# Two graph-attention layers and a binarized layer on one core: new places for three vector and scalar operations within a step, and a third buffer for the 8-bit adjacency blocks

## The chip, the cores and the metric

The kernel runs on one core of a Trainium2 chip. The metric is device time in microseconds (us) of one execution, taken as the median of several runs. A profiled execution of the same program gives the trace that the prediction is read from. Engines are named as the profile names them: PE (TensorE; PEld is its weight load), DVE (VectorE), ACT (ScalarE), POOL (GpSimd), SP (the queue that issues most DMAs).

## The reference

`x` has 3327 rows of 512 numbers, `adj` is a 3327 by 3327 matrix of zeros and ones. Two graph-attention layers run one after the other, then layer norm, then a layer on signs, then layer norm again.

```python
def _gat_layer(x, W, adj):
    proj = x @ W
    Wh, Ws = jnp.split(proj, 2, axis=-1)
    scores = Wh @ Ws.T
    a = jax.nn.softmax(scores, axis=-1) * adj
    out = a @ Wh
    out = out + x
    return jax.nn.leaky_relu(out, NEG_SLOPE)
...
# layer 0: x = layernorm(x + gat(gat(x)));  layer 1:
bw = sign(weight); ba = maximum(sign(x), 0)
out = relu(adj @ (ba @ bw.T))
x = layernorm(x + out)
```

## The kernel before

**Tiling.** The 3327 rows make 26 tiles of 128, taken in pairs: 13 pairs. An attention layer is a walk over 169 steps `(g, q)`: `g` is the pair of query rows, `q` the pair of key rows. Scores are computed transposed, keys on the 128 partitions, so that a step's block of scores is one tile `s` of 128 x 512 (two halves of 128 x 256). The function `attention` (L707) is called once for each of the two layers (`l` 0 and 1).

**What a step does.** The loop over `v` (L1348) writes the instructions of one step into all queues. A step works on several blocks at once, since the work on a block is a pipeline: scores are computed 31 steps ahead, and in step `v`

- `shift` (L1041, DVE L1044) subtracts the query rows' maximum from the block of step `v+3`. The maximum lies in a PSUM tile, `beside`, which `spread` (L1038, an ACT copy) fills once a group `g`;
- `exponential` (L1046, ACT L1050; for a group's first block also L1049 into `total`) follows on the same block;
- `running` (L1052, DVE L1055) adds the block of step `v+2` to the group's running total; a group's first block needs no addition;
- `masked` (L1057, DVE L1060) multiplies the block of step `v+2` by its adjacency block and calls `sums` (L1088), four subtractions and additions on POOL (L1093 to L1096) that prepare the Strassen-like product;
- `values` (L1104) multiplies the block of step `v` by the values on PE (L1120, 14 matmul instructions);
- `scores` (L881) or `quad_scores` (L786) compute a part of the scores of later blocks on PE;
- each layer also makes an 8-bit copy of half of the adjacency blocks (`narrow` L1063, ACT L1068, into a tile of tag `adj_b` with 2 buffers), counts degrees (`degrees`, POOL L1073), checks that the entries are zeros and ones (`exact`, DVE L1083) and, in the next step, stores the copy (`keep_blocks`, a DMA issued by POOL, L1076). In most of a layer this is every other step; a few places in between take a further block (`room`, L1341), so that there three steps in a row have one.

**The order by hand.** Every piece of a step is put on a list `work` with a place in the step, a number between 0 and 1 (L1370 to L1399), the list is sorted by it (L1400) and written out. The sort sets the order of the instructions on each engine's queue; each engine then works through its queue in order and waits where something is not ready. So a place is no time: it says only what stands ahead of what on the same engine. Places over 1 go to later steps through the table `early`.

**The scores by blocks of 26 products.** For most key rows the scores come from `quad_scores`: one block of 26 products of 128 x 128 by 128 x 256 (L820, two matmul instructions each) for four steps, interleaved with the matmuls of `values`. The products are numbered in `ORDER` and have the places `(n + 0.5) / 6.5` for n = 0 to 25. They accumulate in PSUM banks `P`, `Q`, `R`, later `S`, `T`, `V`; `ps_ch` has three of them. A bank is read out between two products on it, by ACT (`keep_as`, L826, and `seed`, L829, which writes one back) or by DVE (`out`, L832), and the next product on the bank waits for that reading. DVE's readings have the place of their product plus 0.082, ACT's plus 0.03. There are five such blocks in a pass of 26 steps (two groups), five passes of that kind and 25 blocks in each layer. The steps of a block have different readings: in its first step DVE has product 16 (place 0.774), in the second 12 and 9 (0.082 and 0.236), in the third 21, 7, 24, 6 (0.31, 0.467, 0.62, 0.774), in the fourth 15, 18, 5, 10, 17, 2 (0.082, 0.236, 0.39, 0.544, 0.70, 0.852). ACT's readings fall in the first two steps and early in the third. `maximum` (L868, DVE L879) keeps the running maximum over keys, with places such as 0.49 and 0.79. For the first and last key rows of a pass the scores come from `scores` instead, with products on banks `Z`, `Y`, `X` (L781), ACT copies (L897, L902, L926, L930) and DVE additions (L916, L922).

**The maximum over partitions.** `column_max` (L951) folds a group's maximum in five pieces (`fold`, `turn`, `across`, `along`, `back`) that a table of places, `plans` (L937), spreads over steps.

Of the kernel before, what the change touches and what calls it, by code (L numbers as in the profile page):

```python
# [11 lines left out]
F8 = mybir.dt.float8e4  # L12
# [7 lines left out]
P = 128  # L20
# [3 lines left out]
HW = CW // 2  # L24
# [21 lines left out]
def kernel(  # L46
# [24 lines left out]
    def halves_of(c):  # L71
        return [g for g in (2 * c, 2 * c + 1) if g < NQ]

    def dense(c):
        return 0 < c and len(halves_of(c)) == 2 and c < NC
# [20 lines left out]
    def slot(shape, dtype, name):  # L96
        return ring.tile(shape, dtype, tag="s", bufs=SBUFS, name=name)
# [609 lines left out]
    def attention(l, att):  # L707
# [67 lines left out]
        def product(c, q, bank, a, b, start):  # L775

            if start:
                w = len(halves_of(c)) * P
                ch[bank] = ps_ch.tile([P, w], F32, tag="ch", name=f"p{bank}_{l}_{c}_{q}")
            for k in range(2):  # L780
                nc.tensor.matmul(  # L781
                    ch[bank], xs[c, q, a][:, k], query(c, b)[:, k],
                    start=(start and k == 0), stop=(k == 1), skip_group_check=True,
                )
# [96 lines left out]
        def scores(c, q, s):  # L881

            if dense(c) and q // 2 in quads:
                if (q % 2, s) == (0, 0):
                    quad_scores(c, q // 2)
                return []
            mine = halves_of(c)
            if s == 0:
                for i in mine:
                    sc[i, q] = slot([P, 2, HW], F32, f"s_{l}_{i}_{q}")  # L890
            w = len(mine) * P
            lo, hi = sc[mine[0], q][:, :, :w], sc[mine[-1], q][:, :, HW - w :]
            c11, c21, c12, c22 = lo[:, 0], lo[:, 1], hi[:, 0], hi[:, 1]

            def copied(name, bank):
                ch[name] = att.tile([P, w], F32, tag=name, bufs=1, name=f"{name}_{l}_{c}_{q}")
                nc.scalar.copy(ch[name], ch[bank])  # L897

            def z1():
                product(c, q, "Z", A11, B11, True)  # L900
                ch["X"] = ps_ch.tile([P, w], F32, tag="ch", name=f"pX_{l}_{c}_{q}")
                nc.scalar.copy(ch["X"], ch["Z"])  # L902

            def y5():
                product(c, q, "Y", S1, T1, True)
                copied("p5", "Y")

            def z6():
                product(c, q, "Z", S2, T2, False)
                copied("u2", "Z")  # L910

            def y3():
                product(c, q, "Y", S4, B22, False)

            def add12():
                nc.vector.tensor_tensor(c12, ch["Y"], ch["u2"], ALU.add)  # L916

            def z7():
                product(c, q, "Z", S3, T3, False)

            def add22():
                nc.vector.tensor_tensor(c22, ch["Z"], ch["p5"], ALU.add)  # L922

            def x2():
                product(c, q, "X", A12, B21, False)
                nc.scalar.copy(c11, ch["X"])  # L926

            def z4():
                product(c, q, "Z", A22, T4, False)
                nc.scalar.copy(c21, ch["Z"])  # L930

            if s == 1:

                after.append((-0.05, lambda: maximum(mine[0], q)))
                if q == NQ - 1:

                    plans = [  # L937
                        ((1, -0.04), (1, 0.2), (1, 0.6), (2, 0.16), (2, 0.17)) if mine[0] == 0
                        else ((1, -0.04), (1, 0.2), (1, 0.7), (2, 0.02), (2, 0.3)),
                        ((2, 0.68), (5, 0.83), (6, 0.83), (7, 0.83), (8, 0.83)),  # L940
                    ]
                    for i, plan in zip(mine, plans):
                        for (n, at), do in zip(plan, column_max(i)):
                            early.setdefault(v + n, []).append((at, do))
            if s == 0:
                return [(0.06, z1), (0.31, y5), (0.56, z6), (0.81, y3), (0.94, add12)]
            return [
                (0.02, z7), (0.15, add22), (0.35, x2), (0.68, z4),
            ] + [(0.62, lambda i=i: maximum(i, q)) for i in mine[1:]]
# [91 lines left out]
        def shift(g, q):  # L1041
            s = sc[g, q]
            at = beside[l][:, 0:1]
            nc.vector.tensor_tensor(s, s, at.to_broadcast([P, 2, HW]), ALU.subtract)  # L1044

        def exponential(g, q):  # L1046
            if q == 0:
                total[g] = att.tile([P, 2, HW], F32, tag="total", name=f"total_{l}_{g}")
                nc.scalar.activation(total[g], sc[g, q], AF.Exp)  # L1049
            nc.scalar.activation(sc[g, q], sc[g, q], AF.Exp)  # L1050

        def running(g, q):  # L1052

            if q > 0:
                nc.vector.tensor_tensor(total[g], total[g], sc[g, q], ALU.add)  # L1055

        def masked(g, q):  # L1057

            s = sc[g, q]
            nc.vector.tensor_tensor(s, s, adj[g, q], ALU.mult)  # L1060
            sums(g, q, s)

        def narrow(g, q):  # L1063

            t = adj[g, q, "b"] = att.tile(
                [P, 2, HW], F8, tag="adj_b", bufs=2, name=f"ab_{l}_{g}_{q}"
            )
            nc.scalar.copy(t, adj[g, q], saturate=False)  # L1068

# [192 lines left out]
        if last:  # L1262
# [14 lines left out]
            for n, e in enumerate(some):  # L1277
                at = n * (n1 - n0) / len(some)
# [59 lines left out]
        mine = [i for i, e in enumerate(steps) if e[1] % L == l]  # L1338
# [9 lines left out]
        for v in range(-LOOK - 4, len(steps)):  # L1348
            u = v + LOOK

            if 0 <= v + WS - 1 < len(steps):
                load_ws(*steps[v + WS - 1])
            if 0 <= v + 4 < len(steps):
                load_adj(*steps[v + 4])
            if v + 4 in blocks and (v + 4 < 0 or blocks[v + 4] != steps[v + 4]):
                load_adj(*blocks[v + 4])
            if 0 <= u + 2 < len(ahead):
                c, q, h = ahead[u + 2]
                if h == 0:
                    load_xs(c, q)  # L1360
            if u == -4:
                load_gs(0, 0, 7)

            c, i = divmod(u, 2 * NQ)
            if 0 <= c < NC - 1 and 22 <= i < 25:
                load_gs(c + 1, 2 * i - 44, 1 if i == 24 else 2)
            if dense(c) and i == 0 and quads:
                for n, at, do in query_sums(c):
                    early.setdefault(v + n, []).append((at, do))
            work, after = after, []  # L1370
            if 0 <= c < NC - 1 and i == 2 * NQ - 1:
                work += [
                    (at, lambda c=c, n=n: load_gs(c + 1, n)) for n, at in ((5, 0.43), (6, 0.8))
                ]
            if 0 <= v + 3 < len(steps):
                s3 = steps[v + 3]
                if not any(s3):
                    work.append((-0.02, lambda: spread(0)))
                at = 0.12 if v >= 0 else 0.33 if v < -2 else 0.45
                work += [(0.0, lambda: shift(*s3)), (at, lambda: exponential(*s3))]  # L1380
                if s3[1] == NQ - 1 and s3[0] + 1 < NQ:
                    work.append((0.9, lambda: spread(s3[0] + 1)))
            if 0 <= v + 2 < len(steps):
                s2 = steps[v + 2]
                work += [(0.2, lambda: running(*s2)), (0.48, lambda: masked(*s2))]
            if v + 2 in blocks:
                of = blocks[v + 2]
                work += [
                    (0.6, lambda: narrow(*of)), (0.61, lambda: degrees(*of)),
                    (0.66, lambda: exact(*of)),  # L1390
                ]
                after.append((0.5, lambda of=of: keep_blocks(*of)))
            if later and (last or v + 2 not in blocks or len(later) > 5 - v % NQ // 2):
                work += [(0.8, later.pop(0))]
            if 0 <= u < len(ahead):
                work += scores(*ahead[u])
            if v >= 0:
                work += values(*steps[v])
            work += early.get(v, [])  # L1399
            for _, do in sorted(work, key=lambda e: e[0]):  # L1400
                do()
            if v >= 0 and steps[v][1] == NQ - 1:
                later += finish(steps[v][0])
            if last:
                load_products(v)
# [337 lines left out]
```

## Time and profile before

| | us |
|---|---|
| median of 3 runs | 2499.78 (2499.44 to 2500.13) |
| the profiled execution, its own time | 2498.87 |
| span of that execution, first to last instruction | 2497.1 |
| PE busy in the span | 2471.4 |
| DVE busy | 2031.8 |
| POOL busy | 1505.6 |
| ACT busy | 852.9 |

| group | times | mean ns | busy us |
|---|---|---|---|
| L1044 shift, DVE | 338 | 674 | 227.7 |
| L1050 exponential, ACT | 338 | 631 | 213.2 |
| L1055 running total, DVE | 312 | 844 | 263.4 |
| L1060 masking, DVE | 338 | 717 | 242.5 |
| L879 maximum, DVE | 286 | 786 | 224.0 |
| L1068 8-bit copy, ACT | 169 | 617 | 104.3 |
| L1076 its store, issued by POOL | 169 | 556 | 94.0 |

The first table has whole times; the busy time of an engine is the union of its instructions' records. The second has instructions by line; "mean ns" is the mean length of one record. The granted TensorE clock is 0.999 of full speed over the whole execution.

### The profile page before, as it was taken

How to read it: one execution, taken by the hardware profiler on the slowest of the kernel's cores; microseconds unless marked ns; L12 is line 12 of the kernel's file. 1: busy time of each engine (PE TensorE's matmuls, PEld its weight loads, DVE VectorE, ACT ScalarE, POOL GpSimd, SP SyncE). 2: the span in 40 equal slices, each digit the busy share in tenths (PEclk: the TensorE clock that was granted, in tenths of full speed). 3: DMA queues.
4: the chain of work that ended last, by engine and by line, in shares of the span. 5: the costliest groups of instructions: out<-in, count | busy, mean ns of one | idle time of the engine just before them, and what ended most of it. 6: DMA issues, size and time to landing. Idle time of an engine off the chain costs nothing.

```text
span 2497.1 us, 39159 instructions
## 1 busy us (share of the span) xinstructions
PE 2471.4 (99%) x12052; PEld 2140.4 (86%) x12052; DVE 2031.8 (81%) x4005; ACT 852.9 (34%) x2127; POOL 1505.6 (60%) x2487
## 2 busy tenths in 40 slices
PE   9999999999999999999999999999999999999998
PEld 7888888888888888998888888888888888899886
DVE  6864788888988988768886588988889898888876
ACT  3333433333333333322233333333333333332234
POOL 3772566767677676545677256666666666655631
PEclk9999999999999999999999999999999999999999
DMA  6976767676677766897797676767767677688985
GB/s 209 322 267 222 249 236 253 233 262 236 239 253 236 266 230 231 294 317 258 244 334 270 225 260 220 269 223 265 241 232 270 227 268 240 230 283 301 317 279 174
DMA packets 318149, 635.89 MB, mean 255 GB/s; under 512 B 34317, under 2 KB 182405, under 8 KB 317934
## 3 DMA queue, kind: packets, MB, share of 16 engines
q1 hardware_dynamic: 289454, 540.93, 64.9%
q0 software_dynamic: 28480, 92.40, 9.6%
q8 instruction: 98, 1.61, 0.3%
q14 instruction: 117, 0.96, 0.1%
HBM read 521.98 MB, written 111.21 MB: 254 GB/s over the span
## 4 chain that ended last, share of the span: by engine, by line
PE 93%; DVE 4%; DMA 1%; issue 1%; ACT 1%; POOL 0%; SPq 0%; ACTq 0%; DVEq 0%; POOLq 0%
PE acc L1120 38%; PE pZ L781 9%; PE pP L820 6%; PE pQ L820 6%; PE pY L781 5%; PE pR L820 4%; PE pZ_wh L547 4%; PE pZ_g L612 3%; PE agg L1471 3%; PE pX L781 2%; PE pY_wh L547 2%; PE pY_g L612 2%; PE pT L820 2%; PE pS L820 1%; PE pm L439 1%; PE pV L820 1%
## 5 line engine op out<-in xcount | busy, mean ns | idle before, releaser
L1093 POOL TENSOR_TENSOR as<-s 128x128 f32<-128x128 f32 x338 | 210.9, 624 | 563.3 <-DVE s L1060 424.6
L1120 PE MATMUL acc<-ws,s 128*128 128x256 f32 x1352 | 402.3, 379 | 0.0
L1120 PE MATMUL acc<-ws,as 128*128 128x256 f32 x1352 | 380.5, 379 | 0.0
L1120 PE MATMUL acc<-wh,s 128*128 128x256 f32 x1352 | 380.0, 379 | 0.0
L1050 ACT ACTIVATE s<-s 128x512 f32<-128x512 f32 x338 | 213.2, 631 | 399.5 <-DVE s L1044 397.6
L1073 POOL TENSOR_TENSOR deg<-deg,adj 128x256 fp8e4<-128x256 fp8e4 x338 | 263.6, 780 | 44.5 <-DMA adj<-in_adjT_dram 29.7
L1120 PEld LDWEIGHTS acc<-ws,as 128*128 128x128 f32 x1352 | 251.4, 190 | 37.0 <-issue 3.1
L1120 PEld LDWEIGHTS acc<-wh,s 128*128 128x128 f32 x1352 | 252.5, 190 | 32.5
L1120 PEld LDWEIGHTS acc<-ws,s 128*128 128x128 f32 x1352 | 251.4, 190 | 33.1
L1055 DVE TENSOR_TENSOR total<-total,s 128x512 f32<-128x512 f32 x312 | 263.4, 844 | 0.0
L1060 DVE TENSOR_TENSOR s<-s,adj 128x512 f32<-128x512 f32 x338 | 242.5, 717 | 2.6 <-DMA adj<-in_adjT_dram 0.3
L879 DVE TENSOR_TENSOR top<-top,s 128x512 f32<-128x512 f32 x286 | 224.0, 786 | 23.4 <-ACT s L930 21.3
L781 PE MATMUL pZ<-ga,xs 128*128 128x256 f32 (+1 forms) x1096 | 234.3, 340 | 2.1 <-DVE s L922 1.7
L1044 DVE TENSOR_TENSOR s<-s,beside 128x512 f32<-128x512 f32 x338 | 227.7, 674 | 2.5 <-ACT beside L1039 2.5
L1094 POOL TENSOR_TENSOR s<-s 128x128 f32<-128x128 f32 x338 | 207.4, 614 | 26.7
L781 PEld LDWEIGHTS pZ<-ga,xs 128*128 128x128 f32 x1096 | 191.4, 190 | 26.4 <-DVE s L922 2.5
L1095 POOL TENSOR_TENSOR as<-s 128x128 f32<-128x128 f32 x338 | 191.3, 566 | 26.5
L1096 POOL TENSOR_TENSOR as<-s,as 128x128 f32<-128x128 f32 x338 | 185.3, 548 | 26.5
L1120 PE MATMUL acc<-wh,as 128*128 128x256 f32 x676 | 201.2, 379 | 0.0
L826 ACT COPY s<-pP 128x256 f32<-128x256 f32 x200 | 74.3, 372 | 249.6 <-PE pP L820 217.3
L1120 PEld LDWEIGHTS acc<-wh,as 128*128 128x128 f32 x676 | 125.7, 190 | 20.2 <-issue 3.6
L1076 POOL DMA_DIRECT2D adj_d<-ab x169 | 94.0, 556 | 78.5 <-ACT ab L1068 58.0
(274 smaller groups left out, 4969.6 us busy)
## 6 DMA issues: line engine op xcount, KB each, us to landing
ws<-ws_d SPq DMA_DIRECT2D x338, 512.0 KB
adj<-in_adjT_dram SPq DMA_DIRECT2D x351, 256.0 KB
xs<-xq_d SPq DMA_DIRECT2D x100, 832.0 KB
xs<-xs_d SPq DMA_DIRECT2D x82, 512.0 KB
xs<-xs_d SPq DMA_DIRECT2D x82, 384.0 KB
gs_d<-gsp POOLq DMA_DIRECT2D x84, 256.0 KB, 3.8
xq_d<-xq POOLq DMA_DIRECT2D x20, 832.0 KB, 4.7
ga<-gs_d SPq DMA_DIRECT2D x54, 256.0 KB
```

The lines of the kernel that those rows point to most:

```text
L781: nc.tensor.matmul(ch[bank], xs[c, q, a][:, k], query(c, b)[:, k], start=(start and k == 0), stop=(k == 1), skip_group_check=True,)
L820: nc.tensor.matmul(bank[b], xs[c, i, f"x{r}"], right, start=r in begins, stop=True, skip_group_check=True,)
L879: nc.vector.tensor_tensor(top[i], top[i], t, ALU.max)
L1044: nc.vector.tensor_tensor(s, s, at.to_broadcast([P, 2, HW]), ALU.subtract)
L1050: nc.scalar.activation(sc[g, q], sc[g, q], AF.Exp)
L1055: nc.vector.tensor_tensor(total[g], total[g], sc[g, q], ALU.add)
L1060: nc.vector.tensor_tensor(s, s, adj[g, q], ALU.mult)
L1073: nc.gpsimd.tensor_tensor(deg[:, g], deg[:, g], adj[g, q][:, a], ALU.add, saturate=False)
L1093: nc.gpsimd.tensor_tensor(s3, a11, a21, ALU.subtract)
L1094: nc.gpsimd.tensor_tensor(a21, a21, a22, ALU.add)
L1095: nc.gpsimd.tensor_tensor(s2, a21, a11, ALU.subtract)
L1120: nc.tensor.matmul(acc[g][i // 2][:, i % 2], a[i], b[i], start=(q == 0 and i % 2 == 0), stop=(q == NQ - 1), skip_group_check=True,)
```

## The change

Four edits. In `attention`'s step loop `shift` goes from place 0.0 to 0.25, `exponential` from 0.12 (0.33 and 0.45 in the three steps ahead of the first) to 0.75 in all steps, `running` from 0.2 to 0.475, directly ahead of `masked` at 0.48. The tile of the 8-bit copies gets a third buffer. In `plans`, the third piece (`across`) of a layer's first group goes from 0.6 to 0.97 of its step. What is computed is the same.

```diff
-                        ((1, -0.04), (1, 0.2), (1, 0.6), (2, 0.16), (2, 0.17)) if mine[0] == 0
+                        ((1, -0.04), (1, 0.2), (1, 0.97), (2, 0.16), (2, 0.17)) if mine[0] == 0
...
             t = adj[g, q, "b"] = att.tile(
-                [P, 2, HW], F8, tag="adj_b", bufs=2, name=f"ab_{l}_{g}_{q}"
+                [P, 2, HW], F8, tag="adj_b", bufs=3, name=f"ab_{l}_{g}_{q}"
             )
...
-                at = 0.12 if v >= 0 else 0.33 if v < -2 else 0.45
-                work += [(0.0, lambda: shift(*s3)), (at, lambda: exponential(*s3))]
+                work += [(0.25, lambda: shift(*s3)), (0.75, lambda: exponential(*s3))]
                 if s3[1] == NQ - 1 and s3[0] + 1 < NQ:
                     work.append((0.9, lambda: spread(s3[0] + 1)))
             if 0 <= v + 2 < len(steps):
                 s2 = steps[v + 2]
-                work += [(0.2, lambda: running(*s2)), (0.48, lambda: masked(*s2))]
+                work += [(0.475, lambda: running(*s2)), (0.48, lambda: masked(*s2))]
```

## The prediction

> **What bounds the kernel.** I read the page first: span, busy shares, the chain that ended last.
>
> ```profile
> span 2497.1 us, 39159 instructions
> PE 2471.4 (99%) x12052; PEld 2140.4 (86%) x12052; DVE 2031.8 (81%) x4005; ACT 852.9 (34%) x2127; POOL 1505.6 (60%) x2487
> PE 93%; DVE 4%; DMA 1%; issue 1%; ACT 1%; POOL 0%; SPq 0%; ACTq 0%; DVEq 0%; POOLq 0%
> ```
>
> PE sets the end; the three operations that move run on DVE and ACT and count only where PE waits for what stands behind them. So the question is how much PE waits, and the busy share hides that: the record of a matmul lasts longer (379 ns for 128x256) than the distance to the next one. The busy time by window tells it by counts, in the middle of layer 0 and of layer 1.
>
> ```profile
> 312.00:1000.00 688.00, 687.66 (x3193) 603.70 (x3192) 598.51 (x1179) 244.07 (x590) 467.23 (x741) 1.00 0.72 243
> 1500.00:2187.00 687.00, 681.23 (x3129) 588.48 (x3128) 606.68 (x1213) 233.01 (x567) 441.59 (x709) 1.00 0.71 245
> ```
>
> The first window has 3193 matmuls in 688 us, 0.2155 us each. At that rate 687 us hold 3188; layer 1 has 3129. The 59 that are missing are 12.7 us of waits, though PE looks busy for 681.23. That is the sum to be won in layer 1; layer 0's steady part has next to none. The first steps of each layer lose more (the slices 250:312.5 and 1437.5:1500 have 272 and 271 matmuls where 291 fit, some 4.2 us each).
>
> Then the tables of waits, PE's and all engines':
>
> ```profile
> PE pP L820 <- DVE s L832: 2.3, 6, 0.4
> PE pQ L820 <- ACT s L826: 2.2, 2, 1.5
> PE pP L820 <- ACT s L826: 2.0, 2, 1.3
> ...
> ACT s L1050 <- DVE s L1044: 397.6, 197, 6.5
> ACT ab L1068 <- DMA adj_d<-ab: 40.0, 17, 4.4
> ```
>
> PE waits where a score bank has not been read out, by DVE or ACT. ACT stands idle 397.6 us in the exponential until DVE has shifted, and 40.0 us in the 8-bit copy until an earlier store has landed; readings queued behind are late. The timeline shows both ways to PE. First the buffer:
>
> ```profile
> 1667.26 0.59 PE L1120 MATMUL acc<-wh,s 128*128 128x256 f32 x2
> ...
> 1668.43 0.62 ACT L1068 CAST ab<-adj 128x512 fp8e4<-128x512 f32 x1 [4.00 <-DMA adj_d<-ab]
> 1668.96 0.36 ACT L826 COPY s<-pQ 128x256 f32<-128x256 f32 x1
> 1669.38 0.70 PE L820 MATMUL pQ<-gb,xs 128*128 128x256 f32 x2 [1.52 <-ACT s L826]
> ```
>
> ACT sat 4.00 us in the copy for a buffer, then read bank Q at 1668.96, and PE's next product on Q, due 0.43 after 1667.26 (two matmuls), came at 1669.38: 1.69 lost. Then the order on DVE, at the start of the third step of a pass's fourth block, layer 1:
>
> ```profile
> 1541.47 0.67 DVE L1044 TENSOR_TENSOR s<-s,beside 128x512 f32<-128x512 f32 x1
> 1541.50 0.59 PE L820 MATMUL pP<-ga,xs 128*128 128x256 f32 x2
> ...
> 1542.06 1.02 DVE L1055 TENSOR_TENSOR total<-total,s 128x512 f32<-128x512 f32 x1
> ...
> 1543.35 0.41 DVE L832 TENSOR_TENSOR s<-pP,s 128x256 f32<-128x256 f32 x1
> ...
> 1543.81 0.70 PE L820 MATMUL pP<-gb,xs 128*128 128x256 f32 x2 [0.42 <-DVE s L832]
> ```
>
> Product 7 on bank P starts at 1541.50; its sum can be read 0.70 later (1542.20) but DVE first shifts and adds to the running total and reads P at 1543.35. The next product on P is only two pitches of 0.86 behind, due at 1543.22: 0.59 lost.
>
> **The parts.** (a) Third buffer. A copy then waits for the store of three copies ago; with one copy a step that is a step, some 5.8 us, more than the longest wait (4.4). Two waits of PE come of it: 1.69 and, at 2114.00, 0.85 (idle 0.68 and 0.17 of hidden pitch). **-2.5**. The ACT and DVE time freed beside it (DVE idles 21.6 us behind these copies) has no other wait of PE.
>
> (b) Shift to 0.25, exponential to 0.75. On ACT the exponential no longer stands ahead of a step's first readings while DVE is late. Worth: one wait of bank Y (1593.31, 0.67 idle + 0.16) and two of bank Z at the layers' starts (0.35 each): **-1.5**. The two waits of bank P for ACT (2.0 us) get no credit: the product after them waits for DVE's reading of product 16 anyway, whose place stays behind shift, total and masking. Costs: the exponential now stands behind the 8-bit copy (0.6) and ahead of ACT's readings at 0.876 and, a step later, 0.80 and 0.95. Copy and exponential are 1.25 us together; in the first step they run between the results of products 23 and 14, in the second a reading comes 0.2 late of the 1.4 that a bank allows (three pitches 2.58, less 0.70 to the result, 0.37 for the copy, 0.1). A group's first block has 0.63 more: still inside. The exponential ends by the end of its step at worst, the total reads it at 0.475 of the next, 2.7 us later. Nothing: 0; without that slack each exponential that is late would cost its lateness once, on DVE.
>
> (c) Total behind the readings below 0.475. Before masking DVE does the same work as before, so no reading is put later while DVE has a backlog; those below 0.25 gain shift and total (0.60 + 0.60 to 1.0), those from 0.25 to 0.475 the total. At 1541 the change gives: shift to 1542.06, reading of Q to 1542.40, of P to 1542.82, in time. Then total (0.60 to 1.02), masking 0.60, maximum 0.60, so the reading of S starts 1544.54 to 1544.96 and ends 0.42 later, against 1544.94, when S is wanted: 0.1 to 0.5 lost instead, I take 0.3. From a block's first product row to its last takes 22.02 us undisturbed; these fourth blocks take 22.92 in all five passes: 5 x (0.90 - 0.30) = -3.0. First blocks of passes two to five take 22.83 to 23.01, because the readings of 12 and 9 stand behind shift and total and the copies-out of a finished group: both now go ahead, -0.83 x 4 = -3.3. The second and third blocks lose some 3 more in readings 15 and 18, which gain, but reading 10 behind them gets no earlier: 0, bounds 0 and -3. **-6.3**.
>
> (d) Where DVE has no backlog the same order costs. Layer 0, third step of a second block:
>
> ```profile
> 617.57 0.68 DVE L1044 TENSOR_TENSOR s<-s,beside 128x512 f32<-128x512 f32 x1
> 618.16 0.87 DVE L1055 TENSOR_TENSOR total<-total,s 128x512 f32<-128x512 f32 x1
> 619.61 0.42 DVE L832 TENSOR_TENSOR s<-pQ,s 128x256 f32<-128x256 f32 x1 [0.58 <-PE pQ L820]
> 620.54 0.42 DVE L832 TENSOR_TENSOR s<-pP,s 128x256 f32<-128x256 f32 x1 [0.51 <-ACT pQ L829]
> 622.09 0.42 DVE L832 TENSOR_TENSOR qu<-pS,qu 128x256 f32<-128x256 f32 x1
> ```
>
> DVE had shifted and added before the results came and then idled 0.58 and 0.51. Now the total waits behind the reading at 620.54, and total, masking and maximum run as one before that of 622.09. This starts at 622.69 with the total at 0.60, ends 623.11, and PE wants S at 623.29: 0.13 to spare after 0.05 for the signal. The reading after it (622.42) has 0.7 to spare, 0.06 where the check of the entries stands between. With the total at its 1.02 of 1542.06 the first is 0.3 late. 35 blocks have this form (the second to fifth of each five, 40 of 50, less the five above): 0 to 10.5. Nearest row: masking, whose place it joins, has a mean of 717 against the total's 844; so mostly 0.60, and I take **+2**.
>
> A rule of the Trainium skill bears on this: "SBUF — State Buffer", section "SBUF: two separate sides", has DVE operations with two SBUF inputs and GpSimd operations that read SBUF shut each other out for a whole instruction. The trace agrees: the total (both inputs in SBUF) has 664/701/1658 ns as minimum, median and maximum, the shift (one in PSUM) 636/675/690. By it the total runs free where POOL waits for the masking, and (d) would be 0; if POOL's degree count still ran there, (d) would go to its upper end.
>
> (e) `across` moves behind the addition L916 but stays ahead of L922, for which PE waits at 268.18; the work ahead of that is the same: 0. If L922 gained, it would be 0.9 a layer.
>
> The moved pieces issue no DMA; POOL's four sums wait for masking, at most 1.0 later; they have 1.5 steps (8.7 us) to `values` and take 2.4, after 1.6 of degree count. If that cover went, PE would wait for L1096.
>
> **Sum.** -2.5 - 1.5 - 6.3 + 2 = -8.3 us, 2490.6 for the profiled execution's 2498.87. The median lies 0.9 above that execution: 2499.8 - 8.3 = 2491.5. With every bound, 2486 to 2496.
>
> **Rivals.** *All of layer 1's waits go* (0.17): with masking and total in POOL's pause DVE gets shorter too. For it: DVE is 88% busy there, 606.68 of 687. Against: the readings of S and T stay near their limits. -12.7 - 1.5 - 2.0 = 2483.5.
> *Only ACT's waits go* (0.15): the work per step on DVE is unchanged, and a late engine stays late. For it: the same 88%. Against: the row at 1543.35, with total ahead of a ready result. -2.5 - 1.5 = 2495.8.
> *Total and masking as one block make a new wait* (0.18), slower: place, the third and fourth step of every block, readings of S, P and T. Price: with the total at 1.02 or more, 35 x 0.3 in the third step and 20 blocks of layer 1 x 0.4 at reading 10, 18.5, against the gains of 10.3: 2508. It decides from a mean total of about 0.9 in its new place (0.13 to spare, then 10.3 over some 55 places is 0.19 each). For it: the mean of 844 today. Against: POOL idles ahead of masking (424.6 us before L1093).
>
> **Chances.** Forecast 0.50; it and the best case are below 2494.8, the second rival about at it. A measurement here can tell 0.2% (5 us) from none: faster 0.66, same 0.17, slower 0.17. Range 2481 (best case and the starts of the layers) to 2502 (into the slower rival).
>
> **What would show it.** Right: no wait of L1068 for its store; ACT's wait for L1044 mostly gone; fourth blocks near 22.3 us, layer 1's window near 3170 matmuls; L1055 nearer 700 ns. Wrong: PE waits for L832 in layer 0's third steps, with total and masking just ahead; or the first blocks still at 22.9, the gain then being not in the order.

## The result and the profile after

The changed kernel takes 2503.93 us (median of 20 runs, 2501.49 to 2507.16), the kernel before 2499.65 beside it (20 runs, 2497.82 to 2501.62): a ratio of 1.0018, 95% interval 1.0012 to 1.0025. It is slower by 4.3 us, just under the 0.2% of the prediction's bound. The profiled execution took 2501.49. First the page of the changed kernel: span, busy time and count by engine, the chain by engine.

```profile
span 2499.6 us, 39173 instructions
PE 2475.7 (99%) x12052; PEld 2137.2 (86%) x12052; DVE 2038.0 (82%) x4005; ACT 843.2 (34%) x2127; POOL 1507.1 (60%) x2487
PE 91%; DVE 7%; issue 1%; DMA 1%; ACT 0%; SPq 0%; ACTq 0%; DVEq 0%
```

DVE's share of the chain went from 4% to 7%, ACT's from 1% to 0%. The windows (columns: the stretch, its length, busy time and instructions of PE, PEld, DVE, ACT and POOL, clock, DMA share, GB/s) say where:

```profile
312.00:1000.00 688.00, 687.58 (x3175) 598.11 (x3174) 595.63 (x1171) 239.32 (x587) 464.59 (x740) 1.00 0.71 242
1500.00:2187.00 687.00, 684.02 (x3137) 588.42 (x3136) 609.37 (x1219) 229.88 (x566) 446.62 (x710) 1.00 0.71 245
```

Layer 0 lost 18 of its 3193 matmuls (18 x 0.2155 = 3.9 us), layer 1 won 8 (1.7 us), where some 40 were forecast. In the tables of waits, PE's and then all engines', each row has total, times and longest:

```profile
PE pR L820 <- DVE s L832: 4.4, 2, 2.5
PE pT L820 <- DVE s L832: 2.0, 7, 0.7
...
PE pP L820 <- DVE s L832: 1.0, 5, 0.2
```

```profile
POOL as L1093 <- DVE s L1060: 345.8, 204, 10.3
ACT s L1050 <- DVE s L1044: 222.9, 63, 6.5
...
PEld pS L820 <- DVE qu L832: 10.9, 40, 0.5
```

PE has no wait for ACT left and ACT none for the store of an 8-bit copy. The exponential waits 222.9 us in 63 places, before 397.6 in 197. What PE still waits for is DVE; the last row is its weight load on bank S, late for DVE's reading in 40 places. The timeline of the same kind of place as the prediction's last one, the third step of a second block of layer 0 (start, length, engine, line, output and inputs, in brackets the idle time before it):

```profile
622.00 0.42 DVE L832 TENSOR_TENSOR s<-pQ,s 128x256 f32<-128x256 f32 x1 [1.13 <-PE pQ L820]
622.94 0.42 DVE L832 TENSOR_TENSOR s<-pP,s 128x256 f32<-128x256 f32 x1 [0.51 <-ACT pQ L829]
623.28 0.68 DVE L1055 TENSOR_TENSOR total<-total,s 128x512 f32<-128x512 f32 x1
623.99 0.69 DVE L1060 TENSOR_TENSOR s<-s,adj 128x512 f32<-128x512 f32 x1
624.60 0.68 DVE L879 TENSOR_TENSOR top<-top,s 128x512 f32<-128x512 f32 x1
625.20 0.42 DVE L832 TENSOR_TENSOR qu<-pS,qu 128x256 f32<-128x256 f32 x1
...
625.69 0.69 PE L820 MATMUL pS<-ga,xs 128*128 128x256 f32 x2
```

DVE idled 1.13 us ahead of the first row, time in which the total ran before. Now total, masking and maximum run as one ahead of the reading of S, 2.26 behind the start of the reading at 622.94; the prediction had 2.15 (622.69 against 620.54). The difference is between two rows: the total ends at 623.96 and the masking starts behind it, at 623.99, 0.71 after the total; the maximum starts 0.61 after the masking, while this is still being recorded. The product on S is released late: its record has 0.69 instead of 0.59, and the next product row comes 0.95 later instead of 0.86.

The fourth blocks of layer 1, forecast to give -3.0. First two more rows of the kernel before, ahead of those that the prediction shows, then the changed kernel:

```profile
1534.37 0.68 DVE L1055 TENSOR_TENSOR total<-total,s 128x512 f32<-128x512 f32 x1
...
1536.33 0.42 DVE L1147 TENSOR_TENSOR h<-acc,op 128x256 f32<-128x256 f32 x1 [0.95 <-ACT op L1146]
```

```profile
1540.36 0.42 DVE L1147 TENSOR_TENSOR h<-acc,op 128x256 f32<-128x256 f32 x1 [0.46 <-ACT op L1146]
1540.70 0.68 DVE L1055 TENSOR_TENSOR total<-total,s 128x512 f32<-128x512 f32 x1
1541.41 0.69 DVE L1060 TENSOR_TENSOR s<-s,adj 128x512 f32<-128x512 f32 x1
...
1545.52 0.59 PE L820 MATMUL pP<-ga,xs 128*128 128x256 f32 x2
...
1546.22 0.67 DVE L1044 TENSOR_TENSOR s<-s,beside 128x512 f32<-128x512 f32 x1
1546.82 0.41 DVE L832 TENSOR_TENSOR s<-pQ,s 128x256 f32<-128x256 f32 x1
1547.15 0.40 DVE L832 TENSOR_TENSOR s<-pP,s 128x256 f32<-128x256 f32 x1
```

Shift starts 0.70 after product 7 (1545.52); before it was 0.03 ahead of it. The reading of P came forward only from 1.85 to 1.63 after the product, not to the 0.9 forecast. The timelines name the total of the step before: it ran at 1534.37, ahead of the take-out L1147 (an addition that empties a bank of a finished group), where DVE idled 0.95 us. Now it stands behind the take-out (1540.70), in a chain of DVE work that has no gap up to the shift, and the chain is longer by its 0.71. All five fourth blocks look alike. No run moves this one total alone. In e4_total_mid (below), where it runs ahead of the take-out again, the shift starts 0.03 behind product 7, but there the third step's own total (1.02 us) stands ahead of the readings, and P is read 1.91 behind the product.

For the account below, each of the 50 blocks is cut at the starts of its 26 product rows; a distance beyond the undisturbed 0.86 (1.29 behind product 4) is a loss, and it is named by the product that it starts from. Mean time from a block's first to its last row, by place in the pass of five:

| mean us, blocks 1 to 5 | layer 0 | layer 1 |
|---|---|---|
| before | 22.25 22.01 22.01 22.19 22.23 | 22.74 22.58 22.60 22.92 22.08 |
| changed | 22.45 22.19 22.11 22.41 22.37 | 22.45 22.55 22.18 23.02 22.37 |
| e4_total_mid (below) | 22.51 22.03 22.04 22.19 22.06 | 22.21 22.07 22.01 22.99 22.21 |

The 22.51 holds one block that ran in part at half the granted clock (see the end of the experiments); without it the mean would be about 22.2.

### The profile page after: what moved, and what is told of

It reads as the page before. It is cut to its first block, busy times and chain, and to the rows that moved or that the text cites. A ratio compares the mean times of both kernels' runs of the same rounds, so it can differ in the third digit from the quotient of the medians.

```text
span 2499.6 us, 39173 instructions
## 1 busy us (share of the span) xinstructions
PE 2475.7 (99%) x12052; PEld 2137.2 (86%) x12052; DVE 2038.0 (82%) x4005; ACT 843.2 (34%) x2127; POOL 1507.1 (60%) x2487
## 4 chain that ended last, share of the span: by engine, by line
PE 91%; DVE 7%; issue 1%; DMA 1%; ACT 0%; SPq 0%; ACTq 0%; DVEq 0%
PE acc L1120 38%; PE pZ L781 9%; PE pP L820 6%; PE pQ L820 6%; PE pY L781 5%; PE pR L820 4%; PE pZ_wh L547 4%; PE pZ_g L612 3%; PE agg L1470 3%; PE pX L781 2%; PE pY_wh L547 2%; PE pT L820 2%; PE pY_g L612 2%; PE pS L820 1%; PE pm L439 1%; DVE total L1055 1%
## 5 line engine op out<-in xcount | busy, mean ns | idle before, releaser
L1093 POOL TENSOR_TENSOR as<-s 128x128 f32<-128x128 f32 x338 | 210.9, 624 | 566.8 <-DVE s L1060 345.8
L1050 ACT ACTIVATE s<-s 128x512 f32<-128x512 f32 x338 | 213.3, 631 | 224.2 <-DVE s L1044 222.9
L1073 POOL TENSOR_TENSOR deg<-deg,adj 128x256 fp8e4<-128x256 fp8e4 x338 | 249.3, 738 | 45.1 <-DMA adj<-in_adjT_dram 30.3
L1060 DVE TENSOR_TENSOR s<-s,adj 128x512 f32<-128x512 f32 x338 | 256.3, 758 | 11.6 <-DMA adj<-in_adjT_dram 0.9
L1055 DVE TENSOR_TENSOR total<-total,s 128x512 f32<-128x512 f32 x312 | 241.4, 774 | 0.1
L1095 POOL TENSOR_TENSOR as<-s 128x128 f32<-128x128 f32 x338 | 198.5, 587 | 26.5
L1096 POOL TENSOR_TENSOR as<-s,as 128x128 f32<-128x128 f32 x338 | 192.3, 569 | 26.5
```

What stands on the lines that cost most here:

```text
L1073: nc.gpsimd.tensor_tensor(deg[:, g], deg[:, g], adj[g, q][:, a], ALU.add, saturate=False)
L1093: nc.gpsimd.tensor_tensor(s3, a11, a21, ALU.subtract)
L1095: nc.gpsimd.tensor_tensor(s2, a21, a11, ALU.subtract)
```

## The experiments

Ratios are to the kernel before, run on the same chip; its medians there were 2499.31 to 2500.45, so a difference of medians can be off by 1 us.

| kernel | median us | ratio, 95% interval |
|---|---|---|
| changed | 2503.93 | 1.0018 (1.0012 to 1.0025) |
| e1_buffer | 2497.62 | 0.9992 (0.9983 to 1.0001) |
| e6_exp_only | 2499.04 | 0.9995 (0.9986 to 1.0004) |
| e10_two_buffers | 2497.06 | 0.9991 (0.9982 to 1.0000) |
| e8_across_back | 2504.95 | 1.0020 (1.0011 to 1.0029) |
| e2_total_early | 2492.49 | 0.9973 (0.9963 to 0.9983) |
| e4_total_mid | 2491.67 | 0.9968 (0.9956 to 0.9980) |
| e3_total_only | 2519.20 | 1.0077 (1.0063 to 1.0091) |
| e5_max_between | 2505.46 | 1.0024 (1.0015 to 1.0034) |
| e11_check_later | 2505.42 | 1.0024 (1.0013 to 1.0034) |
| e7_first_block | 2490.26 | 0.9960 (0.9946 to 0.9974) |
| e9_layer0_only | 2489.50 | 0.9956 (0.9942 to 0.9969) |

**One part alone.** The kernel before with the third buffer:

```diff
-                [P, 2, HW], F8, tag="adj_b", bufs=2, name=f"ab_{l}_{g}_{q}"
+                [P, 2, HW], F8, tag="adj_b", bufs=3, name=f"ab_{l}_{g}_{q}"
```

> The kernel before with only the third buffer. Theory A (the order costs, the buffer helps): the two waits of PE behind the 8-bit copy (1.69 and 0.85 us in layer 1) go, 2.5 us faster than before, 1 to 4. Rival B (the buffer's waits are hidden by later ones): 0 within 1 us.

2497.62, by the ratio 2.0 us below before, though the interval just includes no change. In its trace the third block of layer 1's second pass went from 24.04 to 22.25, the second block of the fifth pass from 23.39 to 22.44, and PE's last instruction starts 2.6 earlier: term (a) as forecast.

The kernel before with the exponential at 0.75 alone:

```diff
-                at = 0.12 if v >= 0 else 0.33 if v < -2 else 0.45
+                at = 0.75
```

> The kernel before with only the exponential moved to 0.75 in all steps (shift stays at 0.0, total at 0.2, two buffers). The move of shift and exponential together, with the third buffer and the total early, was worth about 5 us more than the buffer. Theory E (ACT's waits make it): 3 to 5 us faster than before. Theory S (DVE's readings ahead of the shift make it): 1 to 2 us faster.

2499.04: about 1 us or nothing. The exponential's place alone does not make the gain, though in its trace the first blocks of layer 1's passes two to five already take 22.52 to 22.70 us instead of 22.83 to 23.01.

The kernel before with both, shift at 0.25 and exponential at 0.75, and still two buffers. `across` stands at 0.97 in this run, not at 0.6 as the expectation has it (e8_across_back, below, finds nothing in that edit):

```diff
-                        ((1, -0.04), (1, 0.2), (1, 0.6), (2, 0.16), (2, 0.17)) if mine[0] == 0
+                        ((1, -0.04), (1, 0.2), (1, 0.97), (2, 0.16), (2, 0.17)) if mine[0] == 0
...
-                at = 0.12 if v >= 0 else 0.33 if v < -2 else 0.45
-                work += [(0.0, lambda: shift(*s3)), (at, lambda: exponential(*s3))]
+                work += [(0.25, lambda: shift(*s3)), (0.75, lambda: exponential(*s3))]
```

> The kernel before with shift at 0.25 and exponential at 0.75, and nothing else: two buffers, total at 0.2, across at 0.6. Theory A (the parts add up): the shift's move is worth what e2_total_early (-6.9) has beyond the buffer (-2.1) and the exponential alone (-0.7), so about -4: 2494 to 2496, first blocks of layer 1's passes two to five near 22.24 and its second ones near 22.0, but the wait for the store of the 8-bit block still there. Theory B (the exponential now stands behind the copy that waits up to 4.4 us for its store, and the total waits for the exponential): part of that is lost again, 2496.5 to 2499, with waits of DVE in the total for ACT.

2497.06. Nearly all blocks are those of e2_total_early, the same kernel with three buffers; two are not: the third of layer 1's second pass (24.35 against 22.02) and the second of its fifth (26.63 against 22.01). The timeline of e10_two_buffers in the first of them:

```profile
1666.78 0.62 ACT L1068 CAST ab<-adj 128x512 fp8e4<-128x512 f32 x1 [4.03 <-DMA adj_d<-ab]
1667.31 0.62 ACT L1050 ACTIVATE s<-s 128x512 f32<-128x512 f32 x1
1667.84 0.35 ACT L826 COPY s<-pQ 128x256 f32<-128x256 f32 x1
1668.24 0.70 PE L820 MATMUL pQ<-gb,xs 128*128 128x256 f32 x2 [2.07 <-DMA adj<-in_adjT_dram]
```

The copy waits for its store as before, and now the exponential stands between it and the reading of Q (0.53 more). PE's row names a load, but the reading of Q ended at 1668.19, 0.05 ahead of it: that is what it waited for. So theory B holds, though the waits are PE's for ACT and not DVE's in the total. In the second of the two blocks PE waits 2.66 us, and behind that wait the granted clock is 0.50 from 2111.59 to 2115.01, which makes some 1.7 of its 4.6 us. The parts do not add up: by the ratios the buffer is worth 2.0 us in the old order and 0.0018 of the time, 4.5 us, in the new one. The intervals alone would not tell these two apart; the traces do, where the two blocks lose 2.7 us for want of the buffer in the old order and 7.0 in the new.

The changed kernel with `across` back:

```diff
-                        ((1, -0.04), (1, 0.2), (1, 0.97), (2, 0.16), (2, 0.17)) if mine[0] == 0
+                        ((1, -0.04), (1, 0.2), (1, 0.6), (2, 0.16), (2, 0.17)) if mine[0] == 0
```

> The changed kernel with the third piece of the first group's column maximum back at 0.6. The prediction priced this edit at nothing: within 1 us of 2503.9. Rival: the edit carries up to 1 us a layer, 2 us slower or faster.

2504.95, the same as the changed kernel within their intervals: term (e) is nothing that these runs can tell. In the traces all blocks but the first of each layer agree to 0.3 us in sum; the two first ones take 1.7 and 2.1 us longer in e8_across_back, with a granted clock of 0.50 for 3.41 us in each (see below).

**The place of the total.** The changed kernel with the total back at 0.2, or at 0.26, directly behind the shift:

```diff
-                work += [(0.475, lambda: running(*s2)), (0.48, lambda: masked(*s2))]
+                work += [(0.2, lambda: running(*s2)), (0.48, lambda: masked(*s2))]
```

> The changed kernel with the running total back at place 0.2 (shift stays at 0.25, exponential at 0.75). Theory A (the total directly ahead of masking makes PE wait at products 19 to 21 and 25 of each block, some 11 us): these waits go, 4 to 9 us faster than before. Rival B (shift and exponential at their later places are the loss): slower than before by 2 us or more.

```diff
-                work += [(0.475, lambda: running(*s2)), (0.48, lambda: masked(*s2))]
+                work += [(0.26, lambda: running(*s2)), (0.48, lambda: masked(*s2))]
```

> The changed kernel with the running total at 0.26, just behind the shift: behind the readings at 0.082 and 0.236, ahead of those from 0.31 on. Theory A: the first blocks of layer 1 keep their gain, the third steps lose nothing: 6 to 11 us faster than before. Rival B: slower than before by 2 us or more.

2492.49 and 2491.67, both faster than before. Taken by itself the total's move to 0.475 costs 2503.93 - 2491.67 = 12.3 us and turns a gain into a loss. The windows of e4_total_mid:

```profile
312.00:1000.00 688.00, 688.00 (x3197) 604.83 (x3196) 598.94 (x1179) 241.57 (x594) 474.37 (x745) 1.00 0.71 243
1500.00:2187.00 687.00, 684.12 (x3169) 599.14 (x3168) 615.10 (x1228) 233.05 (x574) 456.45 (x720) 1.00 0.72 247
```

Both layers have more matmuls than in the changed kernel, 22 and 32. Between the two profiled executions (2499.6 and 2490.2 us) the changed one loses 7.4 us in the distances of products 19, 15 and 18, around the readings of S and P behind the third step's masking, in 40 blocks; 4.5 in a block's last distance, of product 2, ahead of product 0 on T, which waits for the reading of product 10 behind the fourth step's masking; it wins 2.2 in the distance of product 24, most of it in layer 1's fourth blocks. What is left nearly cancels: the changed one loses 3.3 more between blocks, the other 2.6 ahead of its first block and 0.8 in it.

The other way round, the kernel before with nothing but the total moved:

```diff
-                work += [(0.2, lambda: running(*s2)), (0.48, lambda: masked(*s2))]
+                work += [(0.475, lambda: running(*s2)), (0.48, lambda: masked(*s2))]
```

> The kernel before with only the running total moved to 0.475. Theory A: the waits at products 19 to 21 and 25 as in the changed kernel, without what the shift's move and the buffer give: 5 to 9 us slower than before. Rival B: within 2 us of before.

2519.20, 19.8 us more than before and more than expected. With shift ahead of a step's first readings and two buffers there is less room for it: layer 1's first three blocks go from 22.74, 22.58, 22.60 to 23.28, 23.15, 22.99. So in these two orders the size differs and the sign does not.

**Why the total is in the way.** Two mechanisms were in question: that the masking, which overwrites the block that the total reads, has to wait for the total's end (the 0.71 above), or that the total now uses loaded time of DVE instead of idle time. The changed kernel with the maximum between total and masking:

```diff
-                place_ = ((4.79, 5.49, 5.79, 6.49) if i < NQ // 2 - 1 else (4.35, 4.79, 5.35, 5.79))[n]
+                place_ = ((4.79, 5.478, 5.79, 6.478) if i < NQ // 2 - 1 else (4.35, 4.79, 5.35, 5.79))[n]
```

> The changed kernel with the maximum at 0.49 moved to 0.478, between total and masking, in the third step of a block (and from 5.49 to 5.478 in the second). Theory G (masking directly behind the total must wait until the total has ended, 0.72 us from start to start where other pairs take 0.60, and that 0.12 uses up the slack): the waits at products 19 to 21 shrink by about 0.1 in each of some 40 third steps, 3 to 4 us faster than the changed kernel's 2503.9. Rival H (the block's sheer length): within 1 us of 2503.9.

2505.46, no gain. The timeline of e5_max_between in a third step shows why:

```profile
363.04 0.67 DVE L1055 TENSOR_TENSOR total<-total,s 128x512 f32<-128x512 f32 x1
363.64 0.68 DVE L879 TENSOR_TENSOR top<-top,s 128x512 f32<-128x512 f32 x1
364.24 0.68 DVE L1060 TENSOR_TENSOR s<-s,adj 128x512 f32<-128x512 f32 x1
364.84 0.41 DVE L832 TENSOR_TENSOR qu<-pS,qu 128x256 f32<-128x256 f32 x1
365.07 0.45 POOL L1093 TENSOR_TENSOR as<-s 128x128 f32<-128x128 f32 x1 [2.37 <-DVE s L1060]
365.18 0.89 DVE L1083 SCALAR_TENSOR_TENSOR dull<-adj 128x512 fp8e4<-128x512 f32 x1
366.00 0.41 DVE L832 TENSOR_TENSOR s<-pP,s 128x256 f32<-128x256 f32 x1
```

All three start 0.60 apart now, and S is read 1.80 behind the start of the total, 0.12 earlier. But the masking ends 0.5 later, POOL's first subtraction, which waits for it, starts just ahead of the check L1083, and this takes 0.89 us instead of the 0.68 that it has in this block of the changed kernel. The reading behind it, of product 6, is late instead. In third steps without a check the loss is gone (distances 0.86 and 0.86) where the total has its usual 0.68. So the check was moved too, behind the reading of product 6:

```diff
-                    (0.66, lambda: exact(*of)),
+                    (0.776, lambda: exact(*of)),
```

> The kernel of e5_max_between (the changed one with the maximum between total and masking), and the check of the entries (DVE L1083) from place 0.66 to 0.776, behind the reading of product 6. In e5 the third steps without a check lost nothing at product 15 (distance to the next row 0.86), those with one still 1.02 to 1.16, where the check took 0.89 to 0.90 us instead of the 0.68 it takes there in the changed kernel, and delayed the reading of product 6 behind it. Theory G (what made the third step late is the masking's wait for the total's end, 0.12, and in e5 the longer check takes its place): the distances at 15 and 18 are 0.86 in nearly all third steps of the second, third and fifth blocks; worth 0.16 to 0.27 in some 18 blocks, 3 to 5 us less than e5: 2500 to 2502.5, at or just below the changed kernel. Theory L (DVE is simply loaded, the order of its pieces matters little): the check's 0.6 to 0.9 only delays the readings 15 and 18 of the fourth step in turn, and the time stays at 2504 to 2508.

In the second, third and fifth blocks 21 of 30 third steps now lose nothing at product 15 (0 in the changed kernel, 5 in e5_max_between): locally theory G is right, and the distances of products 15 and 18 win 6.1 us over e5_max_between. The time is the same all the same, 2505.42: the loss came back at products 22 and 1 of the second step (1.6 in layer 1), 19 (1.6), 5 and 10 (2.0) and 2 (2.0). Theory L is right on the whole. The 0.12 was real, and taking it out of the third steps did not change the time.

**A better version.** In all kernels with the new places the first step of a chunk stays bad. The changed kernel's timeline there:

```profile
278.30 0.67 DVE L1044 TENSOR_TENSOR s<-s,beside 128x512 f32<-128x512 f32 x1
278.90 1.03 DVE L1055 TENSOR_TENSOR total<-total,s 128x512 f32<-128x512 f32 x1
279.96 1.01 DVE L1060 TENSOR_TENSOR s<-s,adj 128x512 f32<-128x512 f32 x1
280.89 0.41 DVE L832 TENSOR_TENSOR s<-pR,s 128x256 f32<-128x256 f32 x1
...
281.36 0.70 PE L820 MATMUL pR<-ga,xs 128*128 128x256 f32 x2 [2.49 <-DVE s L832]
```

The reading that PE waits 2.49 us for stands behind total and masking. On top of e4_total_mid, in the step ahead of a layer's first alone, these and the work on the adjacency block go behind it:

```diff
-                work += [(0.26, lambda: running(*s2)), (0.48, lambda: masked(*s2))]
+                at = (0.78, 0.79) if v == -1 else (0.26, 0.48)
+                work += [(at[0], lambda: running(*s2)), (at[1], lambda: masked(*s2))]
...
+                d = 0.2 * (v == -1)
                 work += [
-                    (0.6, lambda: narrow(*of)), (0.61, lambda: degrees(*of)),
-                    (0.66, lambda: exact(*of)),
+                    (0.6 + d, lambda: narrow(*of)), (0.61 + d, lambda: degrees(*of)),
+                    (0.66 + d, lambda: exact(*of)),
                 ]
```

> The kernel with the total at 0.26, and in the step ahead of the first (v = -1) total, masking, 8-bit copy, degrees and check behind the reading of product 16. The wait of 2.3 us at product 9 of each layer's first block falls to about 0.6: 3 us faster than with the total at 0.26 alone, 2488 to 2490. Rival (masking later makes POOL's sums late for the first values): no faster than 2491.7.

2490.26; layer 0's first block went from 23.61 to 22.22 us, but layer 1's from 22.09 to 23.77. With the edit in layer 0 alone (`v == -1 and l == 0`):

> The kernel of the run e7_first_block, with the later places of a chunk's first step in layer 0 alone. In e7 the first block of layer 1 took 23.77 us from its first product row to its last, against 22.09 in e4_total_mid, its losses standing at products 8 to 10 (2.28 + 0.84 + 0.85); in layer 0 the first block went from 23.61 to 22.22. Theory F (each of the two is the step's own doing): layer 1's first block falls back to about 22.1 and layer 0's stays near 22.2, so 1.7 us less than e7: 2487.5 to 2489.5. Rival (layer 1's first block lost the time elsewhere, behind layer 0's end, so that it only moves): first block of layer 1 still above 23 us, or the gap ahead of it longer, 2490 to 2492.

2489.50, the same as e7 within the intervals. Layer 1's first block still takes 23.78, now without the edit. Neither theory has the reason, which the granted TensorE clock shows. PE there in e9_layer0_only, with one window (the clock is the third number from its end):

```profile
1461.64 0.70 PE L820 MATMUL pR<-ga,xs 128*128 128x256 f32 x2 [2.18 <-DVE s L832]
1462.18 0.59 PE L1120 MATMUL acc<-wh,s 128*128 128x256 f32 x2
1462.61 0.94 PE L820 MATMUL pQ<-ga,xs 128*128 128x256 f32 x2
1463.34 1.06 PE L1120 MATMUL acc<-ws,as 128*128 128x256 f32 x2
...
1463.00:1464.00 1.00, 1.00 (x4) 0.82 (x3) 1.00 (x3) 0.37 (x1) 1.00 (x3) 0.50 0.00 0
```

and in e4_total_mid, which has the same work in the same order at this place:

```profile
1465.82 0.70 PE L820 MATMUL pR<-ga,xs 128*128 128x256 f32 x2 [2.17 <-DVE s L832]
1466.35 0.59 PE L1120 MATMUL acc<-wh,s 128*128 128x256 f32 x2
1466.78 0.59 PE L820 MATMUL pQ<-ga,xs 128*128 128x256 f32 x2
1467.22 0.59 PE L1120 MATMUL acc<-ws,as 128*128 128x256 f32 x2
...
1467.00:1468.00 1.00, 1.00 (x6) 0.90 (x5) 1.00 (x3) 0.37 (x1) 1.00 (x3) 1.00 0.00 0
```

PE waits equally long for the same reading in both. In e9_layer0_only the clock is then 0.50 from 1462.72 to 1466.13, two matmuls take 1.06 us instead of 0.59, and the block is 1.69 longer. In e7_first_block the same happens from 1467.77 on; there the edit only moved PE's wait, from the distance of product 12 (2.34 in e4_total_mid) to that of product 22 (2.28). In e4_total_mid the clock was 0.50 in layer 0's first block instead, from 283.89 to 287.31. Less these 1.7 us its 23.61 is 21.9 (an estimate, half of 3.41 us), so the 22.22 of layer 0 is no gain of the edit itself, unless its shorter wait is what kept the clock up; one execution of each cannot show that. Both kernels beat the one before (by 0.40% and 0.44%) and the changed one, but their intervals overlap that of e4_total_mid: what is shown to be better is the total's place.

The changed kernel's own profiled execution, the fastest of its 20, has no such drop, though PE waits 2.49 and 1.90 us in the two layers' first blocks. Of its 20 executions the seven with a mean granted clock of 0.997 took 2505.35 us on average, the thirteen with 0.998 took 2503.09, so the drops may well be part of the 4.3 us by which it is slower. They are not what the total's place costs: the two profiled executions compared above have none (changed) and one of these drops (e4_total_mid), and the one with the drop is the faster.

## Why the prediction was wrong

The forecast, faster by 8.3 us, has the wrong sign; the third rival has the right one and the right place, though not its condition.

- **(a)** -2.5 held: 2.0 in times, with an interval that just includes nothing, 2.6 in the trace.
- **(b)** is not contradicted in size (-1.5 forecast, about 1 measured and not told from nothing) and was right to give no credit to the two waits of bank P: at 281.36 PE waits for DVE where it had waited for ACT. What it does not say is that the exponential behind the copy needs the third buffer (4.5 instead of 2.0).
- **(c)** had the gain in the right blocks for the shift: e2_total_early, without the total's move, brings layer 1's first blocks of passes two to five to 22.24 (forecast about 22.0), its second to 22.01 to 22.55 and its third to 22.02, where the forecast had 0. Together these blocks are 7.6 us shorter than before, the buffer's part included; the kernel is 6.9 faster. Part of this is the exponential's (e6_exp_only). In the changed kernel itself the first blocks won 1.1 us of the 3.3 forecast: three take 22.46 and the last 23.16. It failed in the fourth blocks: "Before masking DVE does the same work as before, so no reading is put later while DVE has a backlog." That looks at one step. As the timelines read, the total of the step before came out of an idle stretch into the backlog, the shift started 0.70 behind the product, and the blocks took 23.02 us instead of 22.3: +0.5 instead of -3.0. The total's earlier places do not mend these blocks either (22.84 at 0.2, 22.99 at 0.26).
- **(d)** is the step that failed, by its size: +2 for the total's place where DVE has no backlog. It priced three operations at 0.60 each. Total and masking are 0.71 apart, and that took the margin of 0.13: the third steps lose some 0.16 each (5.8 us in the 35 blocks named). The fourth step's masking, which (d) left out and only the rival named, loses 4.5. In all the place 0.475 costs 11.4 us against the old 0.2 (e2_total_early; 12.3 against 0.26), where -1.0 (-3.0 in (c) and +2) was taken. And e11_check_later shows that mending the margin alone wins nothing: the readings that were in time again made others late.
- **The bounds.** (d) gives 0 to 10.5, but "With every bound, 2486 to 2496" does not use its upper end; with it the sum comes to 2500.0, which is no gain.
- **The rival's condition fell.** "It decides from a mean total of about 0.9 in its new place": the mean is 774 ns (844 before), median 683, and the kernel is slower. The Trainium skill's rule in "SBUF — State Buffer", section "SBUF: two separate sides", that DVE operations with two SBUF inputs and POOL operations that read SBUF shut each other out, led to expect a shorter total in the new place: the measured mean agrees, though the masking behind it grew from 717 to 758, and (d) did not go to 0, since the total's length was not what it hung on. The check in e5_max_between, both inputs in SBUF, fits the rule: it takes 0.89 us beside POOL's subtraction against 0.68.
- **(e)** held as far as the runs can tell.
- Of the signs named, the copy's wait went, ACT's wait did not mostly go (222.9 left of 397.6), the fourth blocks (23.02) are on the wrong side, the window of layer 1 has 3137 matmuls of the 3170, and the PE waits behind total and masking in layer 0's third steps, named as what would make it wrong, are there, among the 40 late weight loads of bank S.

## What to carry to other kernels

An operation that runs while its engine would idle is free; moved to "the same work, only later" it is not, and the place it came from has to be followed to the next reading that was only just in time, in the step after too. Parts of a change can have different signs and lean on each other (here the buffer on the exponential's place), so each is worth running alone. A profiled execution is one execution: before a block's time is put down to the order of work, its granted clock wants a look. A margin of 0.1 us wants distances from start to start of just that pair of instructions, not a mean length.

## What was not expected of the hardware

- Two DVE operations of 128x512 f32, one overwriting what the other reads, start 0.717 us apart (median of 310 pairs of total and masking in the changed kernel); shift and total, where the second follows on another block, 0.595 (145 pairs). The second starts about 0.035 behind the end of the first, the independent one 0.08 ahead of it.
- A product row that is released late has a record of 0.69 or 0.70 us instead of 0.59, and costs PE about 0.10 even where the table of waits has no idle time for it.
- Behind a wait of PE of about 2 us the granted TensorE clock was 0.50 for 3.41 us in some cases and not in others. Between 200 and 2400 us the 13 traces have 18 idle stretches of PE of 1.9 us or more, and ten of them (1.96 to 2.66 us) were followed by such a drop, which began 0.06 to 1.31 us after PE had started again; of the other eight the longest was 2.49. There is no drop elsewhere in that stretch. It made a block 1.7 us longer.
